# A two-layer network on one core: the weave gets lags, and GpSimd's queue is put into program order

## The chip, the cores and the metric

The kernel runs on one core of a Trainium2 chip. A core has five engines, each with its own instruction queue: TensorE (PE in the profile, with its weight loads as PEld), VectorE (DVE), ScalarE (ACT), GpSimd (POOL) and SyncE (SP), which here only issues DMAs. TensorE writes to PSUM; VectorE and ScalarE read it from there; GpSimd works on SBUF. The metric is the device time in microseconds of one execution, as the median of several runs.

## What is computed

Input is `x` of 8 sequences x 512 tokens x 128 channels in float32. Two layers follow, each with a modulation (`sa, ca, ga, sb, cb, gb`) from a small product of a condition:

```
# layer 0
h = layernorm(x) * (1 + ca) + sa
xn = layernorm(h)
attn = causal softmax attention, 16 heads of 8            # per sequence
ssm  = conv, silu, x_proj, softplus(dt);
       state h[t] = exp(dt*A) * h[t-1] + (x*dt)*B ;  y = sum_n C*h   # 256 channels x 16 states
h = h + alpha*attn + (1-alpha)*ssm
h = h + ffn(layernorm(h))
x = x + ga * h
h = layernorm(x) * (1 + cb) + sb
x = x + gb * (shared expert(h) + top-2 of 8 experts(h))   # all 8 are computed and weighted
# layer 1
h = layernorm(x) * (1 + ca) + sa
x = x + ga * banded attention over the batch axis, 8 heads of 16
h = layernorm(x) * (1 + cb) + sb
x = x + gb * sigmoid(xr Wr) * (relu(xk Wk)^2 Wv)          # xr, xk mix a token with the one before
```

## The kernel before, in words

Channels lie on the 128 partitions and a sequence's 512 tokens on the free axis; nearly every operation is one 128x512 tile of float32. The eight sequences go through layer 0 one after the other, in a pipeline. While sequence b is in its attention and scan, sequence b-1 is in its feed-forward part and experts, b-2 in layer 1's attention, and b+1 begins.

Each part is a Python generator. It issues some instructions and then yields a number, its cost. `weave` (L200) takes several parts, each with its total cost and the stretch from `begin` to `end` that it is to fill, keeps for each a position that grows by cost x (end - begin) / total, and always goes on with the part whose position is lowest. `alone` runs parts one after the other.

The parts of one sequence's loop (L1004 to L1021) are:
- `attention(b)` (L438): `projections` make `qT` and `kT` of a group of four heads (L465, L472), `maxima` form scores and reduce their row maxima into `mpad` on VectorE (L488, L520), `shifts` transposes the maxima and adds them to `qT` (L534, L539), `exponentials` forms the scores again and takes their exponential on ScalarE (L488, L558), `values` multiplies by the values (L572), and `projected` normalises and projects (L591 to L631).
- `ssm_scan` (L741): in units of two states and 128 channels, 16 units a sequence. ScalarE makes the decays (L750), VectorE a multiply (L783) and two scans (L788), GpSimd multiplies by C (L792), and `add` sums the two states on VectorE (L764) and into `xc` on GpSimd (L765). The product `so` (L806) ends it, and L813 adds it to `h`.
- `head(b+1)` and `after(b+1)`: loading, two norms, and the scan's inputs (L655 to L739).
- `attention2(b-2)` (L302) of layer 1, whose multiplies are on GpSimd (L358, L393) and whose sums are on VectorE.
- `behind`, which is `finish(b-1)`: `tail` (norm, feed-forward, norm), `routing` (L861, small VectorE operations and two exponentials), and `experts` (L934). Each of the nine experts has four products with SiLU (L945, L949) and four that accumulate (L960). VectorE weights the result by `wb`, a row that comes back from DRAM (L957, L968), and GpSimd adds it (L971).

Every norm (`normalised`, L237) is a chain over all engines: product (`_m`, L242), square and copy on ScalarE, product (`_v`, L254), a small VectorE step and a power on GpSimd (`_r`, L263, L264), products that spread the result (`_rb`, L269), a VectorE multiply (L276), and one ScalarE operation (L283).

Two rings of PSUM tiles bind the order. `mm_tile` has three slots for all single products, so a product waits until the tile three places earlier has been read. The scores have two slots of two banks, both of which each call of `products` takes.

Inside `tc.manual_schedule` (L1002) the queues of TensorE, ScalarE and VectorE keep the order in which the program issues. GpSimd's and SyncE's orders are chosen by the scheduler of the framework. `paced` (L221) puts the scan's instructions behind the last VectorE step of attention that `mark` named. After the eighth sequence (from L1025) the last experts are woven with layer 1's mixing (`pair`, `mixing`), and then the rest of layer 1 runs.

Of the kernel before, what the change touches and what calls it, by code (L numbers as in the profile page):

```python
# [17 lines left out]
P = 128  # L18
# [50 lines left out]
MSK, NMSK = _cols(_MASK)  # L69


@with_exitstack
def kernel(
# [126 lines left out]
    def weave(*parts):  # L200

        live = []
        for k, (pieces, whole, begin, end) in enumerate(parts):
            live.append([begin, k, iter(pieces), (end - begin) / whole])
        while live:
            part = min(live)
            cost = next(part[2], None)
            if cost is None:  # L210
                live.remove(part)
            else:
                part[0] += cost * part[3]
# [23 lines left out]
    def normalised(src, name, lane, cost=0.9, n=T, ring=mm_tile, wait=0.0):  # L237


        mps = ring(f"{name}_m")[:, :n]  # L240
        to = mps if len(src.shape) == 2 else mps.rearrange("p (a b) -> p a b", a=src.shape[1])
        nc.tensor.matmul(to, lhsT=centre, rhs=src, start=True, stop=True)  # L242
        yield 0.2
        sq = lnp.tile([P, T], F32, tag=f"ln_s{lane}", name=f"{name}_s")
        nc.scalar.activation(sq[:, :n], mps, AF.Square)
        d = lnp.tile([P, T], F32, tag=f"ln_d{lane}", name=f"{name}_d")[:, :n]
        nc.scalar.copy(d, mps)
        yield 2 * cost - 0.2


        vps = ring(f"{name}_v")
        blocks = [(k, min(k, n - P)) for k in range(0, n, P)]
        for j, (_, lo) in enumerate(blocks):
            nc.tensor.matmul(  # L254
                vps[:, j : j + 1],
                lhsT=sq[:, lo : lo + P],
                rhs=mean_w,
                start=True,
                stop=True,
            )  # L260
        sd = lnp.tile([P, NTT], F32, tag=f"ln_r{lane}", name=f"{name}_r")
        nj = len(blocks)
        nc.vector.tensor_scalar(sd[:, :nj], vps[:, :nj], EPS, None, ALU.add)  # L263
        nc.gpsimd.tensor_tensor(sd[:, :nj], sd[:, :nj], mhalf[:, :nj], ALU.pow)  # L264
        yield cost + wait

        rps = ring(f"{name}_rb")
        for j, (k, lo) in enumerate(blocks):
            nc.tensor.matmul(  # L269
                rps[:, k : lo + P],  # L270
                lhsT=sd[:, j : j + 1].to_broadcast([P, P]),
                rhs=ident[:, k - lo :],
                start=True,
                stop=True,
            )
        nc.vector.tensor_mul(d, d, rps[:, :n])  # L276
        yield cost
        return d

    def layernorm(dst, src, scale, bias, name, lane, cost=0.9, n=T, ring=mm_tile, wait=0.0):  # L280

        d = yield from normalised(src, name, lane, cost, n, ring, wait)
        nc.scalar.activation(dst, d, AF.Identity, bias=bias, scale=scale)  # L283
        yield cost
# [17 lines left out]
    def attention2(s, at):  # L302
# [6 lines left out]
        for i0 in range(0, NB, 2):  # L309
            ps = mm_tile(f"kv{s}_{i0}")  # L310
            for i in range(2):
                for k in range(2):
                    nc.tensor.matmul(  # L313
                        ps[half(k), 2 * C * i : 2 * C * (i + 1)],
                        lhsT=hT[:, (i0 + i) * U : (i0 + i + 1) * U],
                        rhs=cwb("qkv")[:, C:],
                        start=True,
                        stop=True,
                    )
            nc.vector.tensor_add(  # L320
                kv[:, i0 : i0 + 2, :, :].rearrange("p i k c -> p i (k c)"),
                ps.rearrange("p (i c) -> p i c", i=2),
                bias[:, :, C:].to_broadcast([P, 2, 2 * C]),
            )
            yield 0.9
# [13 lines left out]
        yield 0.9  # L339
        yield from paced(attended(s, at, q, kv))  # L340

    def attended(s, at, q, kv):
# [13 lines left out]
        for i in range(NQ):  # L356
            pr = at.tile([P, NB, C], F32, tag="pr", name=f"pr{s}_{i}", bufs=2)
            nc.gpsimd.tensor_mul(  # L358
                pr, kv[:, :, 0, :], q[:, i, :].unsqueeze(1).to_broadcast([P, NB, C])
            )  # L360
            if last:
                summed(last)
            last = i, pr
            yield 1.6
# [8 lines left out]
        yield 1.6  # L373
# [16 lines left out]
        for i in range(NQ):  # L390
            pr = at.tile([P, NB, C], F32, tag="pr", name=f"pv{s}_{i}", bufs=2)
            s4 = [P, NB, H1, D1]
            nc.gpsimd.tensor_mul(  # L393
                pr.rearrange("p j (h d) -> p j h d", d=D1),
                kv[:, :, 1, :].rearrange("p j (h d) -> p j h d", d=D1),
                sc[:, i, :, :].unsqueeze(3).to_broadcast(s4),
            )
            if last:
                gathered(last)
            last = i, pr  # L400
            yield 1.6
# [20 lines left out]
    with ExitStack() as l0:  # L422
# [15 lines left out]
        def attention(b):  # L438
# [23 lines left out]
            def projections(g):  # L462
# [15 lines left out]
                yield 0.9  # L478
# [29 lines left out]
            def maxima(g, step):  # L508
# [19 lines left out]
                yield 0.6 + 0.25 * c0 / P  # L528

            def shifts(g):  # L530
# [10 lines left out]
                yield 1.2  # L541
# [3 lines left out]
            def exponentials(g, step):  # L545
# [15 lines left out]
                yield 0.6 + 0.25 * c0 / P  # L561
# [23 lines left out]
            def projected(g):  # L585
# [14 lines left out]
                yield 0.9  # L600
# [11 lines left out]
                yield 0.9  # L612
# [20 lines left out]

            yield from projections(0)
            for k in range(len(STEPS)):
                yield from maxima(0, k)
            for g in range(NG):
# [3 lines left out]
                )  # L641
                for k in range(len(STEPS)):
                    yield from exponentials(g, k)
                    next(others, None)
                    if g + 1 < NG and k:
                        alone(maxima(g + 1, k - 1))
                    values(g, k)
                    yield 0.85 + 0.25 * k
                    next(others, None)
                if g + 1 < NG:  # L650
                    yield from maxima(g + 1, len(STEPS) - 1)
                alone(others)
            yield from projected(NG - 1)

        def ssm_inputs(b, xn):  # L655
# [36 lines left out]
            yield 1.8  # L692
# [11 lines left out]
            yield 1.7  # L704
# [6 lines left out]
            for c in range(NDI):  # L711
# [15 lines left out]
                yield 0.9  # L727
# [5 lines left out]
                yield 0.9  # L733
            yield 0.9
# [6 lines left out]
        def ssm_scan(b, h, xc, zs, bc, dt, dtx):  # L741
# [27 lines left out]
            for u, (n0, c) in enumerate(units):  # L769
# [16 lines left out]
                yield 0.3  # L786
                for n in range(NN):
# [5 lines left out]
                    yield 0.3  # L793
                    if n == 0 and summed:
                        add(*summed.pop())
                        yield 0.15
                summed.append((n0, c, hs))
            add(*summed.pop())
            yield 0.15
            for c in range(NDI):  # L800
                nc.gpsimd.tensor_mul(xc[c], xc[c], zs[c])
                yield 0.5
            yield 0.5
# [12 lines left out]
        def head(b):  # L816

            load_x(b)
            yield 0.5
# [6 lines left out]
        def tail(b, h):  # L826
# [13 lines left out]
            yield 3.4  # L840
# [13 lines left out]
            yield 3.4  # L854
# [6 lines left out]
        def routing(b, hm):  # L861
# [5 lines left out]
            yield 0.9  # L867
# [25 lines left out]
            yield 0.9  # L893
            yield 0.9
# [14 lines left out]
            for _ in range(4):  # L909
                yield 0.9  # L910
# [23 lines left out]
        def experts(b, hm, we):  # L934
            acc = wk.tile([P, T], F32, tag="moe", name=f"moe{b}", bufs=1)
            wd = None
            for e in range(NE + 1):
# [13 lines left out]
                yield 3.4  # L951
# [22 lines left out]
                yield 3.4  # L974
# [27 lines left out]
        with tc.manual_schedule(engines={mybir.EngineType.PE, mybir.EngineType.Activation, mybir.EngineType.DVE}):  # L1002
            behind = None
            for b in range(NB):  # L1004
# [3 lines left out]
                parts = [(ahead, 42.7, 0.0, 1.0)]  # L1008
# [5 lines left out]
                if b + 1 < NB:  # L1014
                    parts.append((after(b + 1), 8.0, 0.8, 0.97))
                    ahead = attention(b + 1)
                    parts.append((some(ahead, BEGUN), 7.3, 0.85, 1.0))
                if behind:
                    parts.append((behind, 91.5, 0.0, 1.0))
# [142 lines left out]
            def through(sp):  # L1162
# [7 lines left out]
                (behind, 91.5, 0.0, 1.0),  # L1170
# [207 lines left out]
```

## Time and profile before

| what | value |
|---|---|
| median of 3 runs | 2069.03 us (2065.26 to 2073.69) |
| the profiled execution | 2073.63 us |
| its span in the trace | 2071.8 us, so 1.8 us lie around it |
| mean granted TensorE clock | 0.87 |
| one sequence in the steady part | 228.5 us (of 899.5 to 1128.0) |
| busy in it: PE, DVE, ACT, POOL | 192.9, 172.3, 118.8, 128.8 us |
| first sequence (26 to 231 us) | 205 us, with PE 141.6, DVE 147.5 |
| after the last scan (1800.5 to 2071.8) | 271.3 us, with PE 192.8, DVE 117.5 |

Rows that name a line give the engine, the operation, how often it ran, its busy time and the mean time of one. A row of waits says which engine and line stood idle, for whom, how long in total, how many times, and the longest. "PEclk" is the clock that TensorE was granted, as a share of the full one.

### The profile page before, as it was taken

To read this page: it belongs to the slowest core of one execution; us is meant where nothing else is said; L and a number is where in the kernel's file an instruction comes from. 1 tells how busy PE (TensorE), PEld (TensorE's weight loads), DVE (VectorE), ACT (ScalarE), POOL (GpSimd) and SP (SyncE) were. 2 spreads that over 40 slices of the span, in tenths; PEclk is the share of its full clock that TensorE was granted. 3 is DMA by queue.
4 is the path that set the end of the run, shared out by engine and by line. 5 is a ranking of instruction groups with operands and counts; after the bars stand their busy time and mean duration, and the time that the engine had idled before them with its cause. 6 is when DMAs were issued, how large, how long until landed. Compare 5 with 4: busy or idle time off the path is not lost. (4 is left out here: it accounts for less than half of the span.)

```text
span 2071.8 us, 22824 instructions
## 1 busy us (share of the span) xinstructions
PE 1653.0 (80%) x8762; PEld 795.4 (38%) x8762; DVE 1441.0 (70%) x1648; ACT 985.2 (48%) x1413; POOL 1045.2 (50%) x539
## 2 busy tenths in 40 slices
PE   5765888888798887888789788888788768868864
PEld 3332343434343443334334443334333333344442
DVE  1798688647894798668885889568876889352255
ACT  2532555464544644455445554464536454423432
POOL 1566355535673566444772667355763567331131
PEclk9766789998999988999889898999889989968975
DMA  3220123121222122121212122121312122102200
GB/s 101 78 71 21 53 70 99 52 83 56 82 71 78 46 77 82 46 79 59 94 56 83 54 73 78 47 82 60 98 47 78 57 87 81 50 9 76 71 8 18
DMA packets 67405, 135.32 MB, mean 65 GB/s; under 512 B 7864, under 2 KB 23360, under 8 KB 67168
## 3 DMA queue, kind: packets, MB, share of 16 engines
q1 hardware_dynamic: 66816, 131.51, 20.5%
q10 hardware_dynamic: 288, 1.93, 0.3%
q8 instruction: 69, 1.13, 0.2%
q0 software_dynamic: 192, 0.42, 0.1%
q14 instruction: 40, 0.33, 0.1%
HBM read 129.24 MB, written 4.59 MB: 65 GB/s over the span
## 5 line engine op out<-in xcount | busy, mean ns | idle before, releaser
L788 DVE TENSOR_TENSOR_SCAN hs<-da,hs 128x512 f32<-128x512 f32 x256 | 442.8, 1732 | 6.5 <-DVE hs L783 0.5
L792 POOL TENSOR_TENSOR hs<-hs,bc 128x1024 f32<-128x1024 f32 x128 | 386.7, 3021 | 102.2 <-DVE hs L788 83.9
L945 PE MATMUL e<-hm,we 128*128 128x512 f32 x576 | 315.5, 679 | 84.7 <-DVE wb L968 45.6
L558 ACT ACTIVATE ex<-e 128x768 f32<-128x768 f32 (+1 forms) x192 | 158.8, 879 | 317.4 <-PE e L496 317.0
L765 POOL TENSOR_TENSOR xc<-xc,hs 128x512 f32<-128x512 f32 x112 | 199.1, 1778 | 200.1 <-DVE hs L764 200.1
L960 PE MATMUL e<-eh,we 128*128 128x512 f32 x576 | 272.1, 616 | 0.3
L783 DVE TENSOR_TENSOR hs<-bc,dtw 128x1024 f32<-128x1024 f32 x128 | 249.5, 1949 | 0.0
L949 ACT ACTIVATE eh<-e,vec_sb 128x512 f32<-128x512 f32 x288 | 188.5, 686 | 122.1 <-PE e L945 115.2
L520 DVE TENSOR_REDUCE mpad<-s 128x2 f32<-128x256 f32 (+3 forms) x256 | 193.9, 808 | 39.4 <-PE s L496 39.4
L971 POOL TENSOR_TENSOR moe<-moe,wb 128x512 f32<-128x512 f32 x64 | 94.2, 1472 | 223.8 <-DVE wb L968 223.8
L945 PEld LDWEIGHTS e<-hm,we 128*128 128x128 f32 x576 | 111.6, 214 | 241.2 <-issue 89.3
L488 PE MATMUL e<-qT,kT 32*128 32x512 f32 (+3 forms) x1024 | 135.0, 580 | 81.7 <-DVE qT L539 75.3
L750 ACT ACTIVATE da<-dtu,own 128x512 f32<-128x512 f32 x256 | 169.8, 719 | 12.6 <-POOL dtu L737 12.2
L960 PEld LDWEIGHTS e<-eh,we 128*128 128x128 f32 x576 | 108.5, 198 | 127.3 <-issue 113.8
L968 DVE SCALAR_TENSOR_TENSOR wb<-e,vec_sb,wb 128x512 f32<-128x512 f32 x64 | 47.7, 745 | 150.5 <-DMA wb<-wd 58.4
L488 PE MATMUL s<-kT,qT 32*128 32x128 f32 (+3 forms) x1024 | 134.7, 524 | 10.4 <-DVE mpad L520 5.5
L764 DVE TENSOR_TENSOR hs<-hs 128x512 f32<-128x512 f32 x112 | 93.7, 837 | 37.9 <-POOL hs L792 37.9
L393 POOL TENSOR_TENSOR pv<-kv,sc 128x1024 f32<-128x1024 f32 x32 | 62.2, 1952 | 108.4 <-DVE ao L387 90.6
L496 PEld LDWEIGHTS <-ident_b 128*128 128x128 bf16 x1024 | 63.4, 103 | 138.0 <-issue 131.3
L358 POOL TENSOR_TENSOR pr<-kv,q 128x1024 f32<-128x1024 f32 x32 | 88.5, 2777 | 33.6 <-DVE sc L348 18.6
L488 PEld LDWEIGHTS e<-qT,kT 32*128 32x128 f32 x1024 | 51.2, 214 | 139.3 <-DVE qT L539 84.7
L572 PE MATMUL av<-ex,va 128*32 128x512 f32 (+3 forms) x1024 | 99.1, 478 | 0.0
(277 smaller groups left out, 2488.5 us busy)
## 6 DMA issues: line engine op xcount, KB each, us to landing
bc<-bc SPq DMA_DIRECT2D x128, 512.0 KB, 3.8
we<-in_w_dram SPq DMA_DIRECT2D x144, 256.0 KB, 3.1
wb<-wd SPq DMA_DIRECT2D x64, 256.0 KB, 3.3
xin<-in_x_dram SPq DMA_DIRECT2D x8, 256.0 KB, 2.9
wa_sb<-in_wa_dram ACTq DMA_DIRECT2D x1, 1832.0 KB
kept<-ao SPq DMA_DIRECT2D x14, 128.0 KB, 2.5
ai<-kept SPq DMA_DIRECT2D x56, 32.0 KB, 2.2
out_dram<-xout SPq DMA_DIRECT2D x16, 96.0 KB, 2.3
```

Of the source, the lines that this page charges most:

```text
L488: nc.tensor.matmul(tiles[i // 2][:, i % 2, c0 : c0 + n], lhsT=lhs[quadrant(i)], rhs=rhs[quadrant(i)], start=True, stop=False,)
L520: nc.vector.tensor_reduce(mpad[:, qi, 2 * pr : 2 * pr + 2, HD : HD + 1], tiles[pr][:, :, a : a + n], AX.X, ALU.max, negate=True,)
L558: nc.scalar.activation(t[:, :, :c0], tiles[pr][:, :, :c0], AF.Exp)
L572: nc.tensor.matmul(avs[g][quadrant(i), kj * P :], lhsT=va[:, kj, at : at + 32], rhs=ex[i // 2][:, i % 2, c0 : c0 + n], start=(kj == 0), st ...
L750: nc.scalar.activation(da[:, n, :], dt[c], AF.Exp, scale=A_sb[:, c, n0 + n : n0 + n + 1])
L765: nc.gpsimd.tensor_add(y, y, hs[:, 0, :])
L783: nc.vector.tensor_mul(hs, bcs[0], dtx[c].unsqueeze(1).to_broadcast([P, NN, T]))
L788: nc.vector.tensor_tensor_scan(hs[:, n, :], da[:, n, :], hs[:, n, :], 0.0, ALU.mult, ALU.add)
L792: nc.gpsimd.tensor_mul(hs, hs, bcs[1])
L945: nc.tensor.matmul(ps, lhsT=we1[:, m * P : (m + 1) * P], rhs=hm, start=True, stop=True)
L949: nc.scalar.activation(t, ps, AF.Silu, bias=cv("b1", e * NFF + m))
L960: nc.tensor.matmul(ps, lhsT=we2[:, m, :], rhs=hid[m], start=(m == 0), stop=(m == NFF - 1),)
```

## The change

The change gives `weave` a second number beside the cost. A step may now yield a `Step`: a cost, a lag (how much TensorE work should be issued by others before this part goes on), and `pe`, the TensorE work that it issued itself. `weave` counts the TensorE work issued so far in `now`, and adds 0.06 for each unit of lag that is still open to a part's position when it picks the lowest. Lags are given to the steps of nearly all parts. The steps of the scan have lag 0 and `pe` 0, and so have the later steps of the routing.

Two calls in `attention` that ran `maxima` or the rest of `others` without a pause now yield at each step. In `ssm_scan`, the `add` of the unit before moves from behind the first scan of a unit to behind the second. The total costs of the parts are adjusted to the new sums. The set of engines that keep program order gets GpSimd as a fourth.

The diff, cut to its core; the steps that only turn a plain number into a `Step` are shown by examples.

```diff
+class Step(float):
+    def __new__(cls, cost, lag=0.0, pe=None):
+        self = super().__new__(cls, cost)
+        self.lag, self.pe = lag, cost if pe is None else pe
+        return self
+
+SOON = 0.06
...
     def weave(*parts):
...
-            live.append([begin, k, iter(pieces), (end - begin) / whole])
+            live.append([begin, k, iter(pieces), (end - begin) / whole, 0.0])
+        now = 0.0
         while live:
-            part = min(live)
+            part = min(live, key=lambda p: (p[0] + SOON * max(0.0, p[4] - now), p[1]))
             cost = next(part[2], None)
             if cost is None:
                 live.remove(part)
-            else:
-                part[0] += cost * part[3]
+                continue
+            part[0] += cost * part[3]
+            now += getattr(cost, "pe", cost)
+            part[4] = now + getattr(cost, "lag", 0.0)
...
     def normalised(...):
-        yield 0.2
+        yield Step(0.2, 1.0, 0.9)
...
-        yield 2 * cost - 0.2
+        yield Step(2 * cost - 0.2, 1.8, 0.0)
...
-        yield cost + wait
+        yield Step(cost + wait, 5.0, 0.9)
...
-        yield cost
+        yield Step(cost, 1.6, 0.9)
...
     def attention(b):
...
+            def one(pieces, lag=0.0):
+                for cost in pieces:
+                    yield Step(cost, max(lag, getattr(cost, "lag", 0.0)))
+                    break
...
+                more = 2 * (g + 1 < NG) + (g > 0) * (2 + (g - 1) % 2)
                 for k in range(len(STEPS)):
-                    yield from exponentials(g, k)
-                    next(others, None)
-                    if g + 1 < NG and k:
-                        alone(maxima(g + 1, k - 1))
+                    follows = g + 1 < NG and k
+                    yield from exponentials(g, k, 0.0 if follows or more else 3.2)
+                    yield from one(others, 0.0 if follows else 2.4)
+                    more = max(0, more - 2)
+                    if follows:
+                        yield from maxima(g + 1, k - 1)
                     values(g, k)
-                    yield 0.85 + 0.25 * k
-                    next(others, None)
+                    yield Step(0.85 + 0.25 * k)
+                    yield from one(others, 0.5)
                 if g + 1 < NG:
-                    yield from maxima(g + 1, len(STEPS) - 1)
-                alone(others)
+                    yield from maxima(g + 1, len(STEPS) - 1, 0.8)
+                yield from others
...
     def ssm_scan(...):
-                yield 0.3
+                yield Step(0.3, 0.0, 0.0)
                 for n in range(NN):
...
-                    yield 0.3
-                    if n == 0 and summed:
+                    yield Step(0.3, 0.0, 0.0)
+                    if n == NN - 1 and summed:
                         add(*summed.pop())
-                        yield 0.15
+                        yield Step(0.15, 0.0, 0.0)
...
     def routing(b, hm):
-            yield 0.9
-            yield 0.9
+            yield Step(1.8, 1.5, 0.4)
...
             for _ in range(4):
-                yield 0.9
+                yield Step(0.9, 0.0, 0.0)
...
     def experts(b, hm, we):
-                yield 3.4
+                yield Step(3.4, 2.6)
...
-                yield 3.4
+                yield Step(3.4, 0.8)
...
-        with tc.manual_schedule(engines={mybir.EngineType.PE, mybir.EngineType.Activation, mybir.EngineType.DVE}):
+        with tc.manual_schedule(engines={mybir.EngineType.PE, mybir.EngineType.Activation, mybir.EngineType.DVE, mybir.EngineType.Pool}):
...
-                parts = [(ahead, 42.7, 0.0, 1.0)]
+                parts = [(ahead, 64.3, 0.0, 1.0)]
...
-                    parts.append((after(b + 1), 8.0, 0.8, 0.97))
+                    parts.append((after(b + 1), 9.8, 0.8, 0.97))
...
-                    parts.append((behind, 91.5, 0.0, 1.0))
+                    parts.append((behind, 92.0, 0.0, 1.0))
```

## The prediction

> **What bounds the kernel now.** I read the page's busy table first: no engine is full, TensorE (PE) is nearest.
>
> ```profile
> PE 1653.0 (80%) x8762; PEld 795.4 (38%) x8762; DVE 1441.0 (70%) x1648; ACT 985.2 (48%) x1413; POOL 1045.2 (50%) x539
> ```
>
> Then busy time by stretch, cut at matching points of each sequence's loop (us from the span's start; length, then PE, PEld, DVE, ACT, POOL, granted clock):
>
> ```profile
> 26.00:231.00 205.00, 141.62 (x828) 69.27 (x828) 147.45 (x142) 75.11 (x109) 98.28 (x49) 0.75 0.15 48
> ...
> 671.00:899.50 228.50, 192.88 (x1061) 90.13 (x1060) 172.38 (x192) 118.85 (x164) 128.80 (x65) 0.90 0.22 70
> 899.50:1128.00 228.50, 192.86 (x1057) 90.30 (x1056) 172.33 (x192) 118.81 (x164) 128.79 (x65) 0.90 0.23 70
> ```
>
> The kernel repeats a 228.5 us sequence; in it PE idles 228.5 - 192.9 = 35.6 us. Who ends those idles, in the second of these sequences:
>
> ```profile
> PE e L488 <- DVE qT L539: 9.6, 2, 6.9
> PE e L945 <- DVE wb L968: 6.1, 1, 6.1
> PE lna_rb L269 <- POOL lna_r L264: 4.6, 1, 4.6
> PE ln_rb L269 <- POOL ln_r L264: 4.1, 1, 4.1
> PE e L945 <- ACT eh L949: 3.9, 4, 2.1
> PE lnc_m L242 <- DVE xT L975: 3.4, 1, 3.4
> ```
>
> PE waits because a small VectorE (DVE) or GpSimd (POOL) step of its own chain is late. That step is late because of what stands before it in DVE's strict order, above all the scan part: 249.5 us of multiplies (L783), 442.8 of scans (L788) and 93.7 of adds (L764), together 786 of DVE's 1441 us. So the time is set by two in-order queues, PE and DVE, that feed each other, and a change of order is priced in PE idle time.
>
> An idle also costs after it ends. Slices of 3.4 us around the longest (L539's 6.95 us, at 1076.5 to 1083.5):
>
> ```profile
> 1076.30:1079.70 3.40, 0.22 (x1) 0.00 (x0) 0.54 (x1) 0.00 (x0) 2.83 (x2) 1.00 0.24 77
> 1079.70:1083.10 3.40, 0.00 (x0) 0.00 (x0) 3.22 (x6) 0.00 (x0) 2.73 (x3) 0.82 0.00 0
> 1083.10:1086.50 3.40, 3.03 (x13) 1.36 (x14) 0.97 (x2) 0.58 (x1) 3.40 (x2) 0.50 0.00 0
> 1086.50:1089.90 3.40, 3.40 (x6) 1.12 (x4) 0.00 (x0) 3.25 (x5) 1.43 (x2) 0.68 0.09 34
> ```
>
> The clock falls to 0.50 when PE resumes. The shortfall (0.50 + 0.32) x 3.4 us while PE works is 2.8 us.
>
> **The change, part by part.** No arithmetic is added or removed, only orders move, so instructions cost nothing by themselves. Listing both queues for one repeated sequence (from one `so` to the next) gives what moves.
>
> *Gains* (PE work put between a producer and its reader, by rows of this trace: a 128x512 f32 product 0.93 to 1.1 us, an expert's four 3.6 to 3.7):
> - `qT`: in the fourth group an expert (3.6 us) stood between `mT` and `e`, but the add of `mT` into `qT` sat behind the second attention's softmax on DVE. Now the group comes after `so`, behind other DVE work that fits; 6.95 goes. In the third group nothing stood between, now an expert half does; 2.64 goes.
> - `ln2`: `rb` followed `v` at once (4.1 us waited). Five products and transposes now lie between, so that wait itself is covered; what replaces it is A below.
> - `lna`: 2.8 us between becomes 4.4; 1.6 of 4.6 goes.
> - The `xT` wait (3.4): POOL's last `moe` add now stands before the `dtu`/`dtw` ops, which took it 1.7 us; I take 1.4.
> - The expert's `wb` wait for its DMA (DVE 7.6, PE 6.1): the round trip stays, 2.6 us more PE work lies before it; I take 2.3.
> Sum without `ln2`: 6.95 + 2.64 + 1.6 + 1.4 + 2.3 = 14.9 us.
>
> *Losses.* The scan's steps carry lag 0 and advance no PE time; the others carry lags of 0.5 to 5. One unit of pending lag adds 0.06 to a part's key, and a scan step adds 0.3 x 0.83 / 19.3 = 0.0129 to its own: one unit lets 4.7 scan steps go first. DVE's queue shows it. Runs of scan work with nothing between: before 33 per sequence, the longest 6 steps; after 24, with runs of 8, 6, 6 and three of 4. By mean rows (scan 1732 ns, multiply 1949, add 837) and by the shortest (1192, 1192, about 670), each run in front of a step that PE waits for:
> - A, 8 steps before `ln2_r`: 3 x 1.95 + 4 x 1.73 + 0.73 = 13.5 us (short 9.1). On POOL, now in program order, `ln2_r` moves behind a second `hs` multiply (3.0) and an `xc` add (1.8). That multiply starts with the run's fourth scan, 2.7 us before DVE reaches `ln2_r`; so POOL adds 2.1 and the power 1.6, in all 17.2 (short 12.4). PE has e, v, q, v, transposes, av, k = 7.5 us meanwhile. Wait 9.7 (4.9) for 4.1: +5.6 (+0.8).
> - B, 6 steps before `lnb_d`: 4 x 1.73 + 1.95 + 0.84 = 9.7 (6.6), then the multiply 0.7 and ScalarE's (ACT's) 0.8; PE has 3.7 before `r1`: +7.5 (+4.4).
> - C, 4 steps before `lna_d`: 6.2 (4.2). `lnb_rb` takes the PSUM slot that `lna_d` frees (three slots), with 1.7 us of PE work between: +4.5 (+2.5).
> - D, the router's yields have lag 0, so its two exponentials follow each other on ACT, ahead of the expert's SiLU. From `k2`'s end: 0.8 + 0.25 + 3.3 (13 small DVE ops, as they took at 974.6 to 977.9) + 0.3 + table load 1.28 + 0.69 = 6.6, with 2.8 of PE work; 3.8 less 0.7 now: +3.1.
> - E, 4 steps before the second expert's `wb`, which holds a slot: 0 to 3.7. F, the softmax and scans before the fourth's: 0 to 5.4.
> Sum 29.8 at most, 10.8 at least, middle 20.3.
>
> Net per sequence -4.1 to +14.9, middle +5.4. To this comes the clock. The Trainium skill, TensorE: Matmul & The Clock Gate, Part 1, says that about 3.4 us of idleness gates the clock to half until about 3.4 us of sustained work: 1.7 us lost per long gap. The trace, which decides, shows 2.8. By such slices the clock dips six times in this sequence now; my list of after has A, B, C, D, the DMA one, and E and F: none to two more dips, so 0 to +5.6, middle +2.6 (+1.6 by the page). Taken: **+8 us** per sequence.
>
> The add that moves behind the second scan (L764) spares DVE its wait for the previous `hs` multiply: 37.9 us over the run, but PE does not stand behind it at once (one case a sequence, 4.7 us, just where `so` follows); zero. It also delays the release of `hs`; with three buffers the next writer comes two units later, more than 10 us by means, against 4.8 of POOL work: zero, and 4.7 a sequence if that cover fails. POOL's own new order elsewhere: its waits are 1026 us of idleness that nobody needs, so zero, bounded by rival 3. SP's issues follow their producers: zero, with the same bound.
>
> The whole: five full sequences 40; the second sequence (longest runs 16.2, 15.2, 10.8 against 11.7, 8.6) +8; the eighth +4; the first +3 (runs of 25.9 and 18.8 against 17.7, but no experts behind them); the last 271 us, without scans, -5: experts now lie between the norms' `v` and `rb`, where 7.2 us were waited. Sum +50.
>
> Span 2071.8 + 50 = 2121.8; with the 1.8 us outside it 2123.6 on the scale of the profiled run (2073.6). The median of the three runs is 4.6 below that: **2119 us**.
>
> **Rivals.**
> 1. *Faster: the lags do what they say, and the runs hide.* If scans in a run go at the short 1.2 us, the losses are 10.8 and the gains 14.9: -4.1, and about two clock drops less, -5.6: -9.7 over six sequences and -5 at the end: 2069 - 63 = 2006; with half of that, 2035. For it: the median scan is 1218 ns. Against: multiplies' median is 2218, and POOL's 3.3 us multiply always follows a run's scans. It decides if the 8-step run takes under about 10 us.
> 2. *No difference:* one wait replaces another of its size, since the three PSUM slots hold PE whichever comes late: 2069. Gains and low losses do nearly meet; but then B must vanish.
> 3. *Slower still, through POOL in program order.* A `moe` add behind a 2.8 us `pr` multiply delays the next `wb` load, which waits for it (SP waited 220 us for `moe` adds), then DVE's `wb` and PE: 2 us for each of 64: +128 over the forecast, half of it likely: 2185. Against: both POOL queues have these adds near the same neighbours.
>
> **Numbers.** Forecast 0.60; rival 1 0.25; rival 2 0.09; rival 3 0.06. The forecast alone spans 2085 to 2170. The range 2035 to 2180 reaches half of rival 1 and to rival 3. About 0.5% (10 us) is what a measurement of this kernel tells from no change. Faster 0.26, same 0.11, slower 0.63.
>
> **What would show it.** Right: a sequence of 233 to 240 us; PE waits for `ln2_r`, for `hm` or `r1`, and for `lna_d`'s slot, of 4 us and more; the `qT` wait of 6.95 gone; a clock below 0.90. Wrong: PE idle under 33 us in a sequence, scans near 1.2 us throughout, or a shorter first sequence with its runs of 19 and 26 us.

## The result, and the profile after

The changed kernel takes 2272.7 us (median of 4 runs, 2263.8 to 2274.7), the kernel before 2068.0 us (4 runs). The ratio is 1.098, interval 1.094 to 1.102: slower by 205 us where 50 were forecast. The direction was right, the forecast size was a quarter of the measured one, and the time lies outside the range. The profiled execution has a span of 2272.0 us against 2071.8, so its 200.2 us are what has to be found.

The busy table of the changed kernel answers to the first line shown of before:

```profile
PE 1702.9 (75%) x8762; PEld 802.6 (35%) x8762; DVE 1434.6 (63%) x1648; ACT 998.9 (44%) x1420; POOL 1001.8 (44%) x539
```

PE is busy 49.9 us longer with the same 8762 products, so that much is a lower clock (granted 0.839 against 0.870; the last section has the working); the other 150.3 us are PE idle time. DVE is no busier. Next the stretches, cut at the end of DVE's add of `so` into `h` (L837), one line for the second sequence (b=1) and one for a repeated one (b=4); columns: length, then PE, PEld, DVE, ACT, POOL, granted clock, DMA share, GB/s:

```profile
217.80:465.90 248.10, 184.47 (x1018) 84.33 (x1015) 155.88 (x172) 113.08 (x154) 102.28 (x54) 0.82 0.18 57
967.90:1220.30 252.40, 199.80 (x1058) 90.96 (x1057) 171.85 (x193) 120.47 (x165) 123.87 (x65) 0.86 0.21 63
```

and the same two of the kernel before:

```profile
209.50:406.90 197.40, 164.97 (x954) 78.14 (x958) 146.13 (x166) 106.84 (x148) 107.63 (x53) 0.88 0.23 72
865.00:1093.70 228.70, 193.06 (x1061) 90.49 (x1064) 172.40 (x194) 118.86 (x164) 128.79 (x65) 0.90 0.22 70
```

A repeated sequence took 228.7 us before with PE busy 193.1; now it takes 252.4 with 199.8: 17.0 us more idleness and 6.7 us of clock. The second sequence took 197.4 us before with PE busy 165.0; now 248.1 with 184.5, of which a part is work: 64 more products (1018 for 954) now fall behind the cut. Who ends PE's idles in the repeated one (967.9 to 1220.3; total, times, longest):

```profile
PE e L968 <- DVE wb L991: 14.9, 4, 4.8
PE e L968 <- ACT eh L972: 6.5, 4, 3.7
PE r L888 <- ACT hm L299: 5.7, 1, 5.7
PE lnb_rb L285 <- DVE lna_d L292: 3.9, 1, 3.9
PE k L488 <- DVE ln_r L279: 3.8, 1, 3.8
PE lna_rb L285 <- POOL lna_r L280: 3.4, 1, 3.4
PE lnc_m L258 <- DVE xT L998: 3.0, 1, 3.0
PE kv L329 <- DVE kv L336: 2.7, 1, 2.7
```

The `qT` wait of 9.6 us is gone, and the waits foretold as B, C and D are there, near their sizes. What stands out is `wb` at the top, 14.9 us for 6.1. The second sequence, same view:

```profile
PE r L888 <- ACT hm L299: 15.7, 1, 15.7
PE e L968 <- DVE wb L991: 10.3, 4, 4.2
PE ln_rb L285 <- POOL ln_r L280: 9.5, 1, 9.5
PE lna_rb L285 <- POOL lna_r L280: 7.4, 1, 7.4
PE ln_m L258 <- ACT h L299: 6.1, 1, 6.1
```

The first line can be followed on DVE (timeline: start, length, instruction; neighbours of a kind are merged):

```profile
336.47 3.22 DVE L812 TENSOR_TENSOR_SCAN hs<-da,hs 128x512 f32<-128x512 f32 x2
339.62 0.66 DVE L788 TENSOR_TENSOR hs<-hs 128x512 f32<-128x512 f32 x1
340.20 3.35 DVE L807 TENSOR_TENSOR hs<-bc,dtw 128x1024 f32<-128x1024 f32 x1
343.66 3.21 DVE L812 TENSOR_TENSOR_SCAN hs<-da,hs 128x512 f32<-128x512 f32 x2
346.79 0.66 DVE L788 TENSOR_TENSOR hs<-hs 128x512 f32<-128x512 f32 x1
347.38 3.36 DVE L807 TENSOR_TENSOR hs<-bc,dtw 128x1024 f32<-128x1024 f32 x1
350.84 2.10 DVE L812 TENSOR_TENSOR_SCAN hs<-da,hs 128x512 f32<-128x512 f32 x1
352.86 0.66 DVE L292 TENSOR_TENSOR lnb_d<-lnb_d,lnb_rb 128x512 f32<-128x512 f32 x1
```

Nine steps of scan work, 16.4 us, stand ahead of one 0.66 us multiply; its input was there since PE's `lnb_rb` ended at 338.7. PE waits 15.7 us for what follows it. Just afterwards DVE's queue has no scan work at all. DVE's and GpSimd's scan work alone (instructions on `hs`), in slices of 15 us, then the clock:

```profile
325.00:340.00 15.00, 13.86 (x10) 9.88 (x5) 0.59 0.18 70
340.00:355.00 15.00, 12.72 (x7) 9.52 (x4) 0.53 0.21 70
355.00:370.00 15.00, 0.00 (x0) 0.00 (x0) 0.91 0.06 19
370.00:385.00 15.00, 2.93 (x3) 1.95 (x1) 1.00 0.14 37
...
415.00:430.00 15.00, 14.23 (x9) 8.78 (x4) 0.97 0.25 80
```

Scan work fills DVE while PE starves (PE is busy 0.59 us of 340 to 355), is absent while PE works, and crowds DVE again among the experts.

Where the 200 us lie, by sequence, against the forecast. The last column is an experiment told below (e15: the lags without the two parts that the prediction priced at zero):

| stretch | forecast | changed | lags alone |
|---|---|---|---|
| first | +3 | +8.3 | +1.3 |
| second (b=1) | +8 | +50.7 | +44.6 |
| five repeated | +40 | +118.3 | +39.3 |
| eighth | +4 | +21.2 | +13.5 |
| the last part | -5 | +1.7 | +5.3 |
| sum | +50 | +200.2 | +104.0 |

The first two rows belong together. The changed kernel issues 616 products before the first cut where there were 704, so the first row hides a loss: PE's idle time in it grew from 78.5 to 102.7 us. The two sequences together lost 59.0 us (45.9 with the lags alone) where 11 were forecast. PE's longest wait of the whole run lies in the first:

```profile
PE e L504 <- DVE qT L555: 24.4, 2, 20.6
PE mT L550 <- DVE mpad L536: 19.2, 4, 14.9
```

On DVE twelve steps of scan work (174.6 to 195.2) stand ahead of that `qT`, and ten (113.9 to 130.1) ahead of that `mpad`.

### The profile page after: what moved, and what is told of

It is laid out like the page before. It is cut to its first block, busy times and chain, and to the rows that moved or that the text cites. A ratio compares the mean times of both kernels' runs of the same rounds, so it can differ in the third digit from the quotient of the medians.

```text
span 2272.0 us, 23020 instructions
## 1 busy us (share of the span) xinstructions
PE 1702.9 (75%) x8762; PEld 802.6 (35%) x8762; DVE 1434.6 (63%) x1648; ACT 998.9 (44%) x1420; POOL 1001.8 (44%) x539
## 5 line engine op out<-in xcount | busy, mean ns | idle before, releaser
L816 POOL TENSOR_TENSOR hs<-hs,bc 128x1024 f32<-128x1024 f32 x128 | 334.7, 2615 | 441.5 <-DVE hs L812 280.3
L968 PE MATMUL e<-hm,we 128*128 128x512 f32 x576 | 331.0, 706 | 154.6 <-DVE wb L991 100.8
L812 DVE TENSOR_TENSOR_SCAN hs<-da,hs 128x512 f32<-128x512 f32 x256 | 425.1, 1687 | 7.9 <-DVE hs L807 0.5
L789 POOL TENSOR_TENSOR xc<-xc,hs 128x512 f32<-128x512 f32 x112 | 225.7, 2018 | 169.3 <-DVE hs L788 169.3
L807 DVE TENSOR_TENSOR hs<-bc,dtw 128x1024 f32<-128x1024 f32 x128 | 281.3, 2198 | 0.0
L504 PE MATMUL e<-qT,kT 32*128 32x512 f32 (+3 forms) x1024 | 123.5, 552 | 44.1 <-DVE qT L555 34.6
L588 PE MATMUL av<-ex,va 128*32 128x512 f32 (+3 forms) x1024 | 112.4, 524 | 3.0 <-ACT ex L574 2.9
```

The lines of the kernel that those rows point to most:

```text
L504: nc.tensor.matmul(tiles[i // 2][:, i % 2, c0 : c0 + n], lhsT=lhs[quadrant(i)], rhs=rhs[quadrant(i)], start=True, stop=False,)
L588: nc.tensor.matmul(avs[g][quadrant(i), kj * P :], lhsT=va[:, kj, at : at + 32], rhs=ex[i // 2][:, i % 2, c0 : c0 + n], start=(kj == 0), st ...
L789: nc.gpsimd.tensor_add(y, y, hs[:, 0, :])
L807: nc.vector.tensor_mul(hs, bcs[0], dtx[c].unsqueeze(1).to_broadcast([P, NN, T]))
L812: nc.vector.tensor_tensor_scan(hs[:, n, :], da[:, n, :], hs[:, n, :], 0.0, ALU.mult, ALU.add)
L816: nc.gpsimd.tensor_mul(hs, hs, bcs[1])
```

## The experiments

My theory: the pending lags let scan steps run ahead in bunches, and PE waits behind the bunches. Rivals: GpSimd's program order; the maxima and second projections, now pieces of their own, which block DVE for PE; and, once the first runs were in, the place of the `hs` add. Times are medians. Ratios are to the kernel before, run beside each (2070.6 to 2072.5 us there, 2068.0 beside the changed kernel).

**e1, e2: GpSimd's order.** e1 is the changed kernel, e2 the kernel before, each with only this list altered (names shortened):

```
e1: - engines={PE, Activation, DVE, Pool}   + engines={PE, Activation, DVE}
e2: - engines={PE, Activation, DVE}         + engines={PE, Activation, DVE, Pool}
```

> The changed kernel, but GpSimd's order left to the scheduler as in the kernel before; the other three queues stay exactly as changed. Lags theory (the runs of scan work on DVE make PE wait): no more than 15 us away from the changed kernel, 2258 to 2288 us, with PE's waits for hm (60 us), for wb (101 us) and for lna_d's slot (20 us) each within 10 us of those. POOL theory (the new program order of GpSimd delays moe, hs and the power): back to 2070 to 2130 us, wb waits near 46 us.

> The kernel before, with GpSimd's queue in program order and nothing else. Lags theory: 2058 to 2080 us, no wait of PE for wb, hm or r moved by more than 10 us. POOL theory: 2140 to 2270 us, wb waits of 80 us and more. What the prediction priced at zero is tested by this run.

e1: 2243.8 us, ratio 1.083 (1.080 to 1.086). e2: 2065.6 us, 0.997 (0.996 to 0.998). So the order costs 29 us in the changed weave, and in the old one it saves some 7. Neither theory had this: it is not the bulk, and it is no zero. PE's wait for `wb` is 82.4 us in e1 in place of 100.8; what makes the difference was not followed to one step. Rival 3's path is not the reason: from the end of `wb` on DVE to the start of `moe` on GpSimd pass 0.64 us on average before, 0.82 as changed and 1.00 in e1, the longest where the time is shorter.

**e3, e8: the weight of a lag.**

```
e3: - SOON = 0.06    + SOON = 0.0
e8: - SOON = 0.06    + SOON = 0.02
```

> The changed kernel with the weight of a pending lag at 0 in place of 0.06: parts are again chosen by their share alone, while the new costs, the interleaved maxima, the add behind the second scan and the POOL order stay. In the repeated sequence the longest run of scan work is 9.0 us in place of 13.5, and lnb_d stands behind 2.8 us in place of 9.7. Lags theory: most of the loss goes, 2080 to 2130 us; waits for hm under 15 us, for wb 45 to 70. Rival, that the maxima and the second projections that are now pieces of their own (in place of being issued at once) block DVE for PE: still 2180 to 2260 us, with DVE waiting over 120 us for PE's products ahead of the maxima.

> The changed kernel with the weight of a pending lag at 0.02 in place of 0.06, so one unit lets 1.6 scan steps go first in place of 4.7. Longest run of the repeated sequence 7.4 us, of the second 9.7 (13.5 and 16.2 as changed). If the loss grows with the weight through the runs: 2085 to 2130 us, waits for hm under 20, for wb under 75. If any weight, however small, turns the order over in the same way: above 2180 us.

e3: 2077.7 us, 1.003 (1.001 to 1.004). e8: 2058.5 us, 0.993 (0.992 to 0.995). All the new pieces, the interleaved maxima, the add's place and GpSimd's order together cost 5 us when the lags have no weight; that rival is out. At a third of the weight the kernel is even 13 us faster than before. Windows of e8 for b=3 and 4:

```profile
627.90:850.90 223.00, 191.61 (x1058) 89.49 (x1057) 171.32 (x194) 120.48 (x165) 125.63 (x65) 0.89 0.23 72
850.90:1077.90 227.00, 195.37 (x1058) 90.71 (x1057) 169.67 (x193) 120.36 (x165) 125.79 (x65) 0.86 0.23 70
```

PE idles 31.4 and 31.6 us of a sequence, less than before (35.6), with the longest run at 7.4 us by mean durations in place of 13.5 (8.6 us as it ran, for b=4).

**e5: lags for the scan steps too.**

```
- yield Step(0.3, 0.0, 0.0)      (behind the multiply and each scan)
+ yield Step(0.3, 1.7, 0.0)
```

> The changed kernel, but each multiply and each scan carries a lag of 1.7 us in place of 0, so that a scan step is held back by the one before it as the other parts are. In the repeated sequence lnb_d and lna_d stand behind one step (1.7 us in place of 9.7 and 6.2), and there are 37 runs in place of 24. Lags theory: the waits for hm, lna_d and the larger half of wb's growth go, 2085 to 2150 us. Rival (interleaved maxima): not below 2180 us, since their order stays.

2113.2 us, 1.019 (1.016 to 1.022): 159 of the 205 us go although the weight is still 0.06. PE's wait for `lna_d`'s slot is gone, for `hm` it is 38 us in place of 60, for `wb` 69.6 in place of 100.8. A new wait took part of the gain: the product `so` waits 43.2 us for GpSimd's last `xc` (4.4 as changed). The runs are the larger cause.

**e6, e7: which lags.** e6 sets the five lags of the norms' pieces to 0, e7 all lags but those.

> The changed kernel with the five lags of the norms' pieces at 0, all other lags as changed. In the repeated sequence lnb_d, lna_d and ln2_r then stand behind 2.8, 0 and 5.4 us of scan work in place of 9.7, 6.2 and 13.5, while the experts' wb keep the runs they have in the changed kernel (4.5, 6.2, 1.7, 4.5). Theory 1, each wait comes from the run just ahead of it: the waits for hm, lna_d and ln_r go (some 90 us with the clock's share), wb's stay at 90 to 105, total 2140 to 2190 us. Theory 2, the runs ahead of the norms use up the scans that would fill DVE later, and so starve and then crowd the stretch of the experts: wb's waits fall as well, to 50 to 70, total 2085 to 2125 us.

> The changed kernel with every lag at 0 but the five of the norms' pieces. ln2_r stands behind 9.1 us of scan work in place of 13.5, lnb_d and lna_d behind none in the repeated sequence, the experts' wb as without any lag. Theory 1 (each wait from the run just ahead of it): a wait of 3 to 6 us for ln_r is all that is left in a sequence, 2090 to 2125 us, wb under 60. Theory 2 (the norms' lags bunch the scans for the whole sequence): wb at 70 to 100 and 2130 to 2200 us.

e6: 2167.0 us, 1.046 (1.043 to 1.049); e7: 2116.0 us, 1.024 (1.019 to 1.028). In e6 PE's wait for `hm` falls from 60.5 to 3.4 us, and `wb`'s is 109.7 us: each wait comes from the run just ahead of it, as theory 1 had it. Over e3 the norms' lags alone cost 38 us, the others alone 89, and both together 195. A lag that is pending in one part may lengthen the runs that another part's lag has opened: a repeated sequence (b=4) has its scan work in 32 runs in e3, 30 in e7, 28 in e6 and 24 as changed. That this is the reason is argued, not shown.

**e10, e11: the add's place.** e10 is the kernel before, e11 the changed one:

```
e10: - if n == 0 and summed:         + if n == NN - 1 and summed:
e11: - if n == NN - 1 and summed:    + if n == 0 and summed:
```

> The kernel before, with nothing changed but the place of the hs add: behind the second scan in place of the first. The prediction took zero for it, with 4.7 us a sequence if the release of hs then decides. Zero: 2062 to 2080 us, and DVE's wait of 38 us for GpSimd's hs under 10. If the release decides: 2090 to 2115 us, with DVE's multiply waiting for its hs buffer or for bc. A gain, below 2060 us, if PE did stand behind that wait.

> The changed kernel with the hs add back behind the first scan. Alone, in the kernel before, moving it saved 16 us. If that saving is there in the changed kernel too, putting it back makes it slower: 2282 to 2305 us, with DVE waiting 25 us and more for GpSimd's hs. If the wait is covered by the longer runs, or if in a run of steps the late add delays the release of hs: 2245 to 2278 us.

e10: 2055.7 us, 0.991 (0.989 to 0.993): the move alone saves 16 us, and DVE's idle time before the add falls from 37.9 us to the last number of this group:

```profile
L764 DVE TENSOR_TENSOR hs<-hs 128x512 f32<-128x512 f32 x112 | 130.6, 1166 | 17.9 <-POOL hs L792 17.9
```

e11: 2217.4 us, 1.072 (1.069 to 1.075): in the changed weave the same move costs 55 us. My expectation for this run allowed for a cost of at most some 27. Most of it lies in SyncE's queue. Issues of the changed kernel, at the first `wb` of a repeated sequence (start, length):

```profile
1128.01 0.33 SPq L800 DMA_DIRECT2D bc<-bc  x1
1128.39 0.33 SPq L954 DMA_DIRECT2D wd<-wT_sb  x1
1137.37 0.33 SPq L800 DMA_DIRECT2D bc<-bc  x1
1137.82 0.83 SPq L980 DMA_DIRECT2D wb<-wd  x2
```

and of e11 at the same place:

```profile
1093.07 0.33 SPq L800 DMA_DIRECT2D bc<-bc  x1
1094.06 0.30 SPq L954 DMA_DIRECT2D wd<-wT_sb  x1
1096.15 0.80 SPq L980 DMA_DIRECT2D wb<-wd  x2
```

In the changed kernel the two `wb` loads stand behind a second `bc` load, and that one waits for its tile until GpSimd's multiply by it has ended, at 1137.34:

```profile
1126.86 3.33 POOL L374 TENSOR_TENSOR pr<-kv,q 128x1024 f32<-128x1024 f32 x1
1130.16 2.18 POOL L789 TENSOR_TENSOR xc<-xc,hs 128x512 f32<-128x512 f32 x1
1132.30 1.93 POOL L280 TENSOR_TENSOR ln_r<-ln_r,own 128x4 f32<-128x4 f32 x1
1134.21 3.13 POOL L816 TENSOR_TENSOR hs<-hs,bc 128x1024 f32<-128x1024 f32 x1
```

From `wd` to the first `wb` load pass 9.4 us in the changed kernel, 7.4 in e1, where `pr` does not stand there, and 2.4 in e11, where the `bc` load comes later. DVE then stands waiting for the load, with all its queue behind it:

```profile
1142.75 0.75 DVE L991 SCALAR_TENSOR_TENSOR wb<-e,vec_sb,wb 128x512 f32<-128x512 f32 x1 [7.61 <-DMA wb<-wd]
```

The jam is not new. In the kernel before, a `bc` load stands at the same place (6.4 us from `wd` to `wb`), and DVE waits 58.4 us for the `wb` load in the whole run. The lags alone (e15, next) bring the `wb` loads in front and the wait down to 7.5 us; the add at its new place brings the `bc` load in front again. The wait is 51.4 us as changed, 50.7 in e1, 15.1 in e11.

**e15: the lags alone.** Both edits, e1's and e11's, in one kernel.

> The changed kernel with the hs add back behind the first scan and GpSimd's order left to the scheduler: the lags and new pieces alone. If the two parts add up (55 and 29 us): 2180 to 2198 us, so that 84 of the 154 us that the prediction missed lie in what it priced at zero. If both cure the same wait: 2205 to 2225 us. If the lags alone cost what was predicted for the whole: 2100 to 2130 us.

2182.8 us, 1.055 (1.051 to 1.058). The two parts add up: singly 55 and 29 us, together 90 of the 205. The lags alone cost 110 over the kernel before beside them. But the 90 us arise only with the lags: with their weight at zero both parts and all new pieces together cost 5 us (e3). Two of its five repeated sequences:

```profile
687.30:922.40 235.10, 187.38 (x1058) 87.06 (x1057) 169.37 (x194) 120.31 (x165) 126.71 (x65) 0.91 0.21 68
922.40:1161.70 239.30, 190.86 (x1058) 88.24 (x1057) 169.66 (x194) 120.30 (x165) 126.75 (x65) 0.89 0.21 67
```

All five sum to 1183.4 us against 1144.1 before: +39.3, where the prediction had 40.

**e19: SyncE's queue by itself.** In the changed kernel, all orders of PE, DVE and GpSimd as they are, `wd` and the first two `wb` of a sequence are issued from ScalarE's queue:

```
- nc.sync.dma_start(out=wd, in_=wT)
+ nc.scalar.dma_start(out=wd, in_=wT)
- nc.sync.dma_start(out=wb, ...)
+ (nc.scalar if e < 3 else nc.sync).dma_start(out=wb, ...)
```

> The changed kernel with the wd store and the loads of the first two wb of each sequence issued from ScalarE's queue in place of SyncE's; all orders on PE, DVE and GpSimd stay. If the two parts priced at zero act through SyncE's queue: the time from wd to wb falls from 9.4 us to under 4, DVE's wait for the wb load from 51 us to under 20, and the total by 30 to 70 us, to 2200 to 2242 us. If that wait is covered (PE waits there for other things anyway) or ScalarE's own wait for wd's landing takes its place: 2255 to 2285 us, and the 90 us lie in the collisions of GpSimd's and DVE's steps.

2224.0 us, 1.074 (1.071 to 1.078): 49 us less. DVE's wait for the load, 51.4 us in the changed kernel, is

```profile
DVE wb L991 <- DMA wb<-wd: 8.4, 2, 5.4
```

So up to 49 of the 90 us went through this queue, nearly as much as the add's 55. The 29 us of GpSimd's order did not go through DVE's wait for this load, which e1 leaves as it was. The other 41 us were not traced to one wait. One place in the trace shows part of them: the four steps ahead of `lna_d` take 7.2 us in the changed kernel (1073.15 to 1080.36), 5.1 in e11 (1041.40 to 1046.47), because GpSimd's multiply and `xc` add both fall on DVE's next multiply when the add stands last (3.36 us against 2.22). That this is the rest is argued, not shown.

**e12: whose wait is `wb`?** ScalarE takes each expert's second product out of PSUM (0.69 us each), DVE reads the copy (the line that allocates `eo` is left out):

```
- nc.vector.scalar_tensor_tensor(wb, ps, cv("b2", e), wb, op0=ALU.add, op1=ALU.mult)
+ nc.scalar.activation(eo, ps, AF.Identity, bias=cv("b2", e))
+ nc.vector.tensor_mul(wb, eo, wb)
```

> The changed kernel, but ScalarE copies each expert's second product with its bias out of PSUM (0.75 us each, 64 of them) into a tile of SBUF, and DVE's wb multiply reads that tile: PE's next product no longer stands behind DVE's queue. If PE's wait for wb (101 us) is the price of DVE's scan runs ahead of wb, it goes to under 15 us, no other wait takes over more than half of it, and the total falls by 60 to 130 us: 2140 to 2215 us. If the experts' stretch is bound by DVE's own work (it is full for 45 us there), PE waits for DVE elsewhere instead: 2230 us and more.

2240.5 us, 1.081 (1.077 to 1.085): 32 us, as the second side had it. PE no longer waits for `wb` at all, but for other DVE steps of the same stretch:

```profile
PE e L968 <- DVE ln_d L292: 36.2, 6, 6.7
...
PE e L504 <- DVE mpad L536: 31.0, 7, 9.5
...
PE e L968 <- DVE qT L555: 20.5, 7, 2.9
```

In the changed kernel these three were 10.9, 9.5 and none. DVE's crowded queue sets the price, not the one step in it that holds PE's slot.

**e16: the router's pieces as before** (two plain steps of 0.9 for `Step(1.8, 1.5, 0.4)`, four plain 0.9 for `Step(0.9, 0.0, 0.0)`), all else as changed.

> The changed kernel with the router's pieces as before (two plain ones of 0.9 and four of 0.9, which also count as PE time), so other parts come between its exponentials. The prediction put 3.1 us a sequence on the two exponentials that follow each other. That alone: 2240 to 2262 us, and waits for the experts' SiLU down from 43 to some 25 us. If DVE's starvation in the router makes the crowded stretch after it: 2170 to 2230 us, wb's waits down from 101 to 60 or less. If neither: 2263 to 2285 us.

2255.0 us, 1.090 (1.084 to 1.095): 18 us, 2.5 a sequence, of the order of the prediction's term D, but its four runs spread over 21 us. PE's wait for the SiLU falls from 42.6 to 35.0 us, less far than expected. The router's back-to-back steps are not what crowds the experts.

**Towards a faster version: e13, e14, e17, e18, e20.** All but e17 have the weight at 0.02 and GpSimd's order left to the scheduler. e13 has no more than that; e14 adds e12's copy; e18 adds e5's lag to e14; e20 adds e19's queue to e14. e17 is the kernel before with e10's move and e12's copy.

> The changed kernel with the weight at 0.02 and GpSimd's order left to the scheduler. Program order for GpSimd cost 29 us with the weight at 0.06 and saved 6 us in the kernel before. If its cost comes with the lags as such: 2025 to 2048 us; if it comes with the long runs alone: 2050 to 2070 us.

> As the last one, with the expert's second product taken out of PSUM by ScalarE. PE waited 71 us for wb with the weight at 0.02; if half of it with its share of the clock is gained: 2000 to 2035 us; if the wait only moves to the next DVE step: 2045 us and more.

> The kernel before, with the add behind the second scan and each expert's second product taken out of PSUM by ScalarE, without any lag. With weight 0.02 and lags the copy saved 17 us. If it does the same here: 2033 to 2045 us, and lags earn nothing. If wb's wait (39 us) hardly stands on the path in this order: 2048 to 2062 us.

> Weight 0.02, scheduler's order for GpSimd, ScalarE's copy (2034.6 us so far), and a lag of 1.7 us on each multiply and scan, which breaks runs (longest 6.2 us in place of 7.4; 37 in place of 32 a sequence). If shorter runs still pay at this weight: 2005 to 2028 us. If runs of up to 7 us are covered: 2030 to 2050 us.

> The fastest so far (weight 0.02, scheduler's order for GpSimd, ScalarE's copy; 2034.6 us) with the same change of queue. DVE waited 43 us there for the wb load and some 60 more without a named releaser. If half of it is on the path: 2005 to 2028 us; if not: 2029 to 2045 us.

e13: 2051.3 us, 0.991 (0.988 to 0.994), against e8's 0.993 (0.992 to 0.995): GpSimd's program order costs at most some 7 us at this weight, 29 at the full one, so it is dear only with the heavy lags. e10, without any lag, reached the same 0.991, so at this weight the lags by themselves are not shown to earn anything. e14: 2034.6 us, 0.982 (0.978 to 0.987). e17: 2084.8 us, 1.007 (1.005 to 1.010), slower than e10 by 29, against both expectations: there PE's wait for `wb` (39 us) gives way to one of `mT` for `ln_d` (40.4 us), since `ln_d` stands on DVE behind the `wb` that waits for its load. e18: 2087.5 us, 1.008 (1.005 to 1.011): the lag that saved 159 us at the full weight costs 53 here, with PE waiting 49.2 us for `ln_d` and 51.7 for `mpad`. I expected neither loss; why e18 orders these worse was not followed further. e20: **2009.3 us, 0.970 (0.968 to 0.972)**, the fastest, ahead of both kernels. Its windows for b=3 and 4:

```profile
619.80:838.60 218.80, 190.11 (x1058) 88.86 (x1057) 168.76 (x194) 125.46 (x173) 124.71 (x66) 0.90 0.23 73
838.60:1056.90 218.30, 189.10 (x1058) 88.15 (x1057) 168.60 (x194) 125.39 (x173) 124.84 (x66) 0.91 0.24 73
```

PE idles 28.7 and 29.2 us of a sequence, 6.4 to 6.9 less than before. The queue edit was not tried on the kernel before, which has the same jam, so what the lags themselves earn of these 61 us stays open. With the copy alone they do earn: e14 against e17.

## Why the prediction was wrong

The direction was argued from the right mechanism, and e3, e5 and e8 confirm it: the runs of scan work that the lags let pass. Two steps gave the wrong size, and a third part came out right by luck.

**1. The steps priced at zero: the add's move, "POOL's own new order elsewhere", and "SP's issues follow their producers".** Together these cost 90 us (e1, e11, e15). The add's risk was looked for at the release of `hs` among three buffers; what it moved was which load stands first in SyncE's queue. GpSimd's multiply holds the `bc` tile, the tile holds SyncE, SyncE holds the `wb` load, and the load holds DVE. I listed DVE's and GpSimd's queues and not SyncE's. GpSimd's 1026 us of idleness were read as proof that its order is free; that order cost 29 us in the new weave, by a way that stays open. The gain of 2.3 us at the expert's `wb` wait for its DMA is there at PE (6.1 us before, 3.2 as changed), but DVE's own wait stayed at 7.6 us.

**2. "The second sequence ... +8" and "the first +3".** The second lost 50.7 us, 44.6 with the lags alone; both together lost 59.0 and 45.9. The prediction had the runs in hand (16.2, 15.2 and 10.8 us in the second, 25.9 and 18.8 in the first) and did not cost the steps behind them. By the working of step B, a 16.2 us run ahead of `lnb_d` is 16.2 + 0.7 + 0.8 with 3.7 us of PE work beside it: 14.0; 15.7 was measured. By step A, 15.2 us ahead of `ln2_r` leaves 15.2 + 2.1 + 1.6 - 7.5 = 11.4; 9.5 was measured, for 5.6 before. These two alone come to 20 us in place of the +8. For the first the prediction noted that no experts stand behind the runs; what does stand there are the attention's own `qT` and `mpad`, for which PE waits 20.6 and 14.9 us (7.3 and 5.4 at the most before).

**3. The repeated sequence: right as a sum for the lags alone, but by luck, as terms offset each other.** PE idle in us against before (E and F with the `wb` load; changed is b=4, lags alone b=3 of e15):

| term | predicted, middle | changed | lags alone |
|---|---|---|---|
| `qT` | -9.6 | -9.6 | -9.6 |
| `lna`, `xT` | -3.0 | -1.6 | -0.1 |
| A, `ln2` | +3.2 | +0.5 | +1.9 |
| B, `hm` | +6.0 | +5.7 | +7.3 |
| C, `lna_d`'s slot | +3.5 | +3.9 | +1.0 |
| D, SiLU | +3.1 | +2.6 | +3.9 |
| `wb`: E, F and its load | +2.2 | +8.8 | +3.3 |
| waits that were not listed | 0 | +7.0 | +4.6 |
| sum of idle time | +5.4 | +17.3 | +12.4 |
| PE busy (clock) | +2.6 | +6.7 | -5.7 |

(By the windows the idle time grew by 17.0 and 12.1 us; the sums here are of listed waits.) B holds within its bounds in both and D is near its 3.1; C holds as changed and not with the lags alone; A came out at its low end or just below. The lengths of the runs were right: that of 8 steps took 13.0 us (13.5 by the mean rows, 9.1 by the shortest), that of 6 steps 9.4 (9.7; 6.6). So the choice of mean rows, on which rival 1 hung, was right: scans average 1.69 us, slow and fast ones by turns. But by A's own working 13.0 us give a wait of 9.2, and 4.6 were measured: PE was still busy with `ln_m` and the product before it for the first 2.5 us of the run (1020.9 to 1023.3), which the working left out, and 1.3 us went to another wait. The term for `wb` was too small because I costed two experts and four wait. The unlisted ones are small: `kv` 2.7, `ex` 2.1, `ln_d`, `at`, `xc` and a transpose 1.3 to 1.5 each, less 3.4 of small waits that went; I had looked only for steps behind long runs. The clock term is the least known. The prediction took +2.6 from 2.8 us a gap in the trace; its 1.7 us a gap and +1.6 are its own estimate, worked out from the figures of the page that it names. Measured were +6.7 and -5.7: with the lags alone PE's busy time falls although it idles more, so neither fixed price per gap holds. Of what was to be seen, the sequence of 233 to 240 us is met by e15 (234.5 to 239.3) and not by the changed kernel (248 to 256).

**The eighth and the last part** were guessed: +4 and -5 against +21.2 and +1.7. The 7.2 us waited between `v` and `rb` in the last part did not go (7.3 now), PE's first router product waits 10.1 us for `hm` there (2.1 before), and PE waits 10.2 us for a load of layer 1 (5.0 before).

**The rivals.** Rival 1 fails at its own point, since the 8-step run takes 13.0 us, not under 10. It was one number away all the same: at weight 0.02 the longest run is 7.4 us by mean rows and the kernel is 13 us faster than before. Nor is it length alone: in the kernel before, too, a run of six steps took 12.1 us (1034.0 to 1046.1), but ahead of the second attention's softmax, and PE's longest wait in the 10 us after it is 2.0 us. Rival 2 asked that B vanish; B is 5.7 us. Rival 3 named GpSimd's order, which cost 29 us of the 205, and a path (`moe`) that the times do not bear out.

## What to carry to other kernels

When a change reorders an in-order queue, list every queue, the DMA issuer's too: an engine that idles half the time can still hold a load, and the load can hold an engine that is waited for. A priority that lets cost-free steps overtake must be checked for how many it lets pass at once and where the longest runs fall; cost each run by the step behind it, in every part of the program, also in those that occur once. Parts priced at zero in the old order have to be priced in the new one: the same move of an add saved 16 us in one and cost 55 in the other.

## What the runs showed of the hardware

- A DVE scan of 128x512 took 1.23 us at most with no GpSimd step beside it, and up to 3.29 with one; the 128x1024 multiply 1.22 and 3.38. In the changed kernel all 107 scans and 63 multiplies of the scan that took over 1.8 us lie beside a GpSimd step, and each ends 1.08 to 1.09 us after such a step ended, as if it got to work only then. In the 16.4 us run above:

```profile
339.83 2.64 POOL L816 TENSOR_TENSOR hs<-hs,bc 128x1024 f32<-128x1024 f32 x1 [2.34 <-DVE hs L812]
342.44 2.24 POOL L789 TENSOR_TENSOR xc<-xc,hs 128x512 f32<-128x512 f32 x1
```

These end at 342.47 and 344.68; DVE's multiply ends at 343.55 and its next scan at 345.76. Not every step beside a GpSimd step is slow: 22 scans and 53 multiplies took under 1.3 us. What decides this was not tried apart.
- ScalarE's queue can issue the first `wb` loads without a visible price: its three issues more a sequence did not show up among PE's waits (SiLU wait 42.8 us in e19, 42.6 as changed).
- PE's busy time for the same 8762 products was 1636.9 us in e20, 1653.0 before and 1702.9 as changed. The clock is recorded as 1.0 or 0.5; weighted with it, as far as the records reach (all but 22 us of either), the busy time comes to 1433 us of full clock before and 1426 as changed. The products themselves took no longer, so the 49.9 us, a quarter of the loss, are clock. It is not in proportion to the idle time (e15: 1644.6 us busy with 112 us more idleness than before), and a run's mean clock does not give it either (0.861 in e15, 0.870 before).
